# Attention stacks: constant rows from the input on GpSimd's queue, heads' outputs loaded further apart, projections moved, stores told later

## The chip, the core and the metric

The kernel runs on one core of a Trainium2 chip. A core has five engines that run side by side and meet only at semaphores: TensorE (PE in the profile; PEld is its loading of weights), VectorE (DVE), ScalarE (ACT), GpSimd (POOL) and SyncE (SP), which here only issues DMAs. Each engine takes its instructions in order, so an instruction that waits holds everything behind it on its engine. DMAs issued by SP and by GpSimd are carried out by 16 DMA engines, which all queues share. TensorE writes its results to PSUM, eight banks of 128 x 512 values; the other engines bring them to SBUF.

The metric is the device time of one execution in microseconds (us). The kernel before takes 858.89 us, the median of three runs (857.42 to 860.17).

## What is computed

One transformer block in float32, for 4 batches of 512 rows of 512 values: layer norm, attention with 32 heads of 16 values, causal, with a linear position bias for each head (ALiBi), projection and residual; then layer norm, a gated FFN with 1376 inner values, and residual.

```python
def attn(x):                                  # x: (4, 512, 512), already normed
    qkv = x @ w_attn + b_attn
    q, k, v = jnp.split(qkv, 3, axis=-1)      # each reshaped to (B, S, 32, 16)
    scores = jnp.einsum('bqhd,bkhd->bhqk', q, k) / 16
    bias = slopes[:, None, None] * rel[None, :, :]      # rel = key position - query position
    scores = jnp.where(causal, scores + bias, -inf)
    out = jnp.einsum('bhqk,bkhd->bqhd', softmax(scores), v).reshape(B, S, 512)
    return out @ w_proj + b_proj

def ffn(x):
    return (silu(x @ w_gate.T) * (x @ w_up.T)) @ w_down.T

x = x + attn(layernorm(x))
x = x + ffn(layernorm(x))
```

## The kernel before

**The order of the work is written out by hand.** Every step is put into a heap with a time (`at`, `spread`, `later`), and at the end the steps are taken out in order of that time and emitted. The unit is a slot: ten slots are one pass over one stack. All matmuls keep this order on TensorE, all DMAs keep it on SP, and instructions wrapped in `pin` keep it among themselves on their engine; other instructions of ScalarE, VectorE and GpSimd may be moved by the scheduler. `later(dt, send)` puts a store dt slots behind the step that made its data, so that SP reaches the store when the data is about ready and doesn't stand waiting.

**Stacks.** The attention goes over 32 stacks `su` = 0..31; unit `u = su // 2` is a quarter of a batch's heads (8 heads), and a stack holds 4 of them. A stack is an SBUF tile of 128 x 3 x 1024 values, four of them (`ST`) used in turn. Its planes hold q and k in pieces (rows 0 to 47 of each half of 64), the head's own slope and position rows (48 to 51), constant rows for the causal mask (52 to 63), and row `KM` = 59, into which the negated row maxima of the scores are written. So one matmul gives scores with bias, mask and maximum already in it. `load_stack` (L494) brings the q and k pieces, six DMAs of 128 KB from a DRAM tensor `qd`; `own_rows` (L479) brings the constant rows. Stacks 0 to 3 get these straight from the input `cst` on GpSimd's queue. For later stacks they come by SP, three DMAs each, from a DRAM tensor `cd`, which `load_cd` (L464) fills from `cst` with two DMAs on GpSimd's queue; the second of them is held by a small store of `c` (`gate`) so that it runs at a set point.

**One pass.** `pass_a` (L541) makes scores of a stack about two passes ahead and VectorE takes their row maxima (L557). `to_row` (L582) turns the maxima on TensorE and a DMA of GpSimd (L588) puts them into row `KM`. `pass_b` (L590) starts at slot `10 * su`: 11 fills (scores matmul, exp on ScalarE, L609, and the causal select of the diagonal block on GpSimd, L611), then values times weights in two parts (`av`, at 8.6 and 10.6 slots), and ScalarE's copy `ue` of the result (L631), which is stored to a DRAM tensor `ud`.

**GEMMs beside the passes.** The q and k projections of the next batch (`qk_steps`), its values (`v_steps`) and the output projection of an earlier batch (`proj_steps`) are spread between the matmuls of the passes, so that TensorE has work while VectorE and ScalarE work on scores. Each is 12 matmuls a tile (three products of high and low parts over four blocks of 128).

**Heads' outputs.** For a unit, `head_sums` loads the sums of the weights, `inverses` takes reciprocals and stores them (`rd`), `attn_heads` (L664) loads the unit's result `uc` and the reciprocals, broadcast, `rb`; `scaled_heads` (L674) multiplies them on GpSimd (L677) and splits the product on ScalarE (L680) and VectorE (L681) into `aT`. Four units make a batch, and then come `proj_steps`, four tiles a batch: `xr` is loaded from x, GpSimd adds the bias (L438), VectorE adds the product (L442), and the sum is stored to `x1d`, from which the FFN reads.

**Buffers.** `xt` (rows for a norm), `raw` (weights before their split), `ue`, `uc`, `rb`, `xr` and FFN's `sg` all share one tag, `x`, of nine buffers of 128 x 512 values. `xnT`, `c`, `aT` and `hl` share the tag `t4` of ten buffers. A buffer is free when the last reader of the tile before is done; for a stored tile that is when the store has landed. The Python line of an SP instruction or of a pinned one is often L77, that of the wrapper; the tile's name tells them apart.

The FFN goes over 4 batches and 11 blocks of the inner size, in slots 312 on; TensorE is its only limit.

Of the kernel before, what the change touches and what calls it, by code (L numbers as in the profile page):

```python
# [26 lines left out]
KM = 59  # L27
# [17 lines left out]
    'wp': 158.0,  # L45
# [20 lines left out]
def block_kernel(ctx, tc, x, wqk, wv, bqk, bv, wp, bp, wgu, wgul, wd, cst, out):  # L66
# [240 lines left out]

    cd = dr.tile([76, 4 * S], FR, name="cd")
# [53 lines left out]
    def qk_steps(u, qk):  # L362
# [13 lines left out]
        def done(p):  # L376
# [11 lines left out]
            def send():  # L388
                made.add(("qd", u, qk))
                sp.dma_start(qds[u][2 * qk : 2 * qk + 2].rearrange("n p c -> p n c"), f(c))  # L390
                if u == 3 and qk == 1:
                    load_cd(f(c)[0:1, 0, 0:1])

            later(1.0 if u < 4 else 3.0, send)
# [25 lines left out]
    def proj_steps(b, t):  # L420
# [19 lines left out]
        def done(p):  # L440
            xr = box["xr"]
            dve.tensor_tensor(xr, p, xr, ALU.add)  # L442

            def send():
                sp.dma_start(x1d[r0 : r0 + 128, :], xr)
                made.add(("x1", b, t))

            later(2.5, send)
# [15 lines left out]
    def load_cd(gate):  # L464

        sp.dma_start(f(cd[72:73, 0:1]), gate)
        pool.dma_start(cd[72:76], cst[72:76])
        pool.dma_start(cd[0:64], cst[0:64])

# [9 lines left out]
    def own_rows(su):  # L479
# [3 lines left out]
        for a in range(2):  # L483
            to = planes(st, a)
            if su < 4:
                to = st[64 * a : 64 * a + 64, 0 : 2 + a : 1 + a]
                pin(pool.dma_start(to[48:52], cst[r0 + 4 * a : r0 + 4 * a + 4].rearrange("r (n c) -> r n c", n=2)))
                pin(pool.dma_start(to[52:64], cst[64:76].rearrange("r (n c) -> r n c", n=2)))
            else:
                sp.dma_start(to[48:52], f(cd[r0 + 4 * a : r0 + 4 * a + 4]).rearrange("r (n c) -> r n c", n=2))  # L490
        if su >= 4:
            sp.dma_start(f(st)[KM : KM + 65 : 64, 0], f(cd[72:74, 0 : 2 * S]))

    def load_stack(su):  # L494
# [6 lines left out]
        if su >= 4:  # L501
            own_rows(su)
# [87 lines left out]
    def pass_b(su, t0):  # L590
# [26 lines left out]
        def av(*js):  # L617
# [11 lines left out]
            if js[-1] == NT - 1:  # L629
# [9 lines left out]
                later(3.0, send)  # L639
# [14 lines left out]
    def inverses(u):  # L654
# [7 lines left out]
        later(2.5, send)  # L662
# [34 lines left out]
    def xT_next(b, t0):  # L697
# [6 lines left out]
        else:  # L704
            spread(t0 - 36.0, t0 - 28.0, loads)
            spread(t0 - 22.0, t0 - 4.0, rest)
# [33 lines left out]
    for su in range(NS):  # L740
# [6 lines left out]
        if su + 4 < NS:  # L747
            at(t0 + 9.7, load_stack, su + 4)
    for b in range(B):
# [4 lines left out]
        if b + 1 < B:  # L754
            xT_next(b + 1, 10.0 * (t + PRM["xt"]) if b else 7.6)
            u = 4 * b + 4
            if b < 2:
# [13 lines left out]
    for b, first, gap, p0, p1_ in ((0, 175.5, 2.2, 192.0, 228.0), (1, 248.0, 2.3, 265.0, 290.0), (2, 273.0, 2.5, 291.0, 316.0)):  # L771
        for k in range(4):
            at(first + gap * k, attn_heads, 4 * b + k)
            at(first + 7.5 + gap * k, scaled_heads, 4 * b + k)
# [76 lines left out]
    def ffn(b, times):  # L851
# [5 lines left out]
        spread(t0 - (23.0 if b else 21.0), t0 - 18.0, loads)  # L857
        spread(t0 - 15.5, t0 - 8.0, rest)
# [130 lines left out]
```

## Time and profile before

| | |
|---|---|
| median of three runs | 858.89 us (857.42 to 860.17) |
| the profiled execution | 856.17 us; its span, first to last instruction, 854.4 us |
| PE busy | 822.4 us, so idle 32.0 us |
| of it idle in 0 to 20 us / 60 to 80 / 280 to 300 | 8.0 / 2.3 / 1.8 |
| idle in 380 to 400 / 400 to 420 / 420 to 440 / 440 to 460 | 1.9 / 7.5 / 3.6 / 2.4 |
| mean granted clock of TensorE in these four | 0.83 / 0.87 / 0.79 / 0.91 |
| VectorE, ScalarE, GpSimd busy | 474.8 / 358.7 / 228.5 us |
| VectorE's row maxima, L557: 512 reductions and 512 reads | 245.9 + 72.5 us |
| ScalarE's exp, L609 | 352, 191.7 us |
| DMA | 99.54 MB, 116 GB/s over the span |
| st<-cd on SP | 84 issues; 56 of 32 KB and 28 of 8 KB |
| st<-mt on GpSimd | 32 issues of 8 KB, 5.5 us to landing |

How to read it: times in the trace count from the first instruction. A stack's maxima row (st<-mt) marks the passes: 69.35, 80.30, 91.43 us and so on stand at slots 10.6, 20.6, 30.6; slot 100.6 is at 176.3 us, 200.6 at 298.7, 250.6 at 368.0 and 300.6 at 446.5. A pass takes 11 us where the GEMMs beside it are thin and 13 to 15 where they are dense. In a list of waits the columns are the engine and line that waited, what it waited for, the sum, the count and the longest, all in us. In an order of time they are start, duration, engine, line, operation and, in brackets, the idle time before it and what ended it. The granted clock is that of TensorE as a share of its full speed.

### The profile page before, as it was taken

The numbers are of one execution on the slowest core, as the hardware profiler recorded it, in microseconds if no ns is written. First come the engines' busy times: TensorE is split into PE (matmuls) and PEld (weight loads), VectorE is DVE, ScalarE is ACT, GpSimd is POOL, SyncE is SP. The second block draws the span as 40 slices with busy tenths as digits, with TensorE's granted clock in tenths as the row PEclk, the third lists the DMA queues.
The fourth block names the chain that finished last, engine by engine and source line by source line (L and its number), as shares of the span: only waits on it lengthen the run. The fifth ranks groups of instructions, "written<-read, shape, count | busy, mean of one in ns | idle before, by whom it ended". The sixth has DMA issues, their size and how long they took to land.

```text
span 854.4 us, 13257 instructions
## 1 busy us (share of the span) xinstructions
PE 822.4 (96%) x4448; PEld 630.6 (74%) x4448; DVE 474.8 (56%) x1438; ACT 358.7 (42%) x678; POOL 228.5 (27%) x519
## 2 busy tenths in 40 slices
PE   6999999999999999999499999999999999999998
PEld 4876777777777577757366788878887888878886
DVE  6798897778877776667384554443114311431112
ACT  4646666566667555555266632221112111121111
POOL 5824443333445443344463211000000000000000
PEclk9999999999999999998799999999999999999999
DMA  6586886578867776668654543312000210110101
GB/s 234 126 184 122 180 183 125 102 153 190 182 141 176 191 171 153 161 153 180 189 164 137 191 122 124 139 37 84 16 25 25 74 25 12 25 63 13 37 1 50
DMA packets 53990, 99.54 MB, mean 116 GB/s; under 512 B 12954, under 2 KB 13210, under 8 KB 53730
## 3 DMA queue, kind: packets, MB, share of 16 engines
q1 hardware_dynamic: 52194, 96.80, 45.6%
q0 software_dynamic: 1728, 1.89, 1.1%
q8 instruction: 36, 0.59, 0.3%
q14 instruction: 32, 0.26, 0.1%
HBM read 65.61 MB, written 33.33 MB: 116 GB/s over the span
## 4 chain that ended last, share of the span: by engine, by line
PE 89%; DMA 3%; ACT 2%; issue 2%; DVE 1%; POOL 1%; SPq 0%; ACTq 0%; POOLq 0%; DVEq 0%
PE bank L85 87%; PE bank L88 2%; DMA ud<-ue 1%; ACT P L609 1%; DMA rb<-rd 1%; DMA xt<-in_x 1%; DMA st<-mt 1%; POOL P L611 0%; POOL uc L677 0%; DVE r L139 0%; ACT c L379 0%; DVE r L77 0%; DVE xt L144 0%; SPq L77 0%; ACT L879 0%
## 5 line engine op out<-in xcount | busy, mean ns | idle before, releaser
L557 DVE CUSTOM_DVE_ANT_0 bank<-bank,mask_t 128x128 f32<-128x128 f32 (+3 forms) x512 | 245.9, 507 | 81.3 <-PE bank L85 75.3
L85 PE MATMUL bank<-xnT,wf 128*128 128x512 f32 (+1 forms) x1056 | 258.5, 393 | 0.0
L85 PE MATMUL bank<-st 128*128 128x512 f32 (+3 forms) x896 | 240.6, 343 | 13.9 <-ACT ue L631 12.6
L609 ACT ACTIVATE P<-bank 128x512 f32<-128x512 f32 (+1 forms) x352 | 191.7, 560 | 115.3 <-PE bank L85 109.0
L85 PEld LDWEIGHTS bank<-xnT,wf 128*128 128x128 f32 (+1 forms) x1056 | 195.5, 186 | 45.3 <-issue 0.2
L85 PEld LDWEIGHTS bank<-st 128*128 128x128 f32 x896 | 159.8, 192 | 43.2 <-ACT ue L631 13.5
L611 POOL TENSOR_SCALAR_AFFINE_SELECT P<-P 128x128 f32<-128x128 f32 (+2 forms) x352 | 123.2, 353 | 186.6 <-ACT P L609 180.2
L883 DVE TENSOR_TENSOR sg<-sg,bank 128x512 f32<-128x512 f32 (+1 forms) x44 | 30.3, 688 | 196.4 <-PE bank L85 195.3
L85 PE MATMUL bank<-xnT,wqk_t 128*128 128x512 f32 x384 | 139.4, 402 | 0.0
L85 PE MATMUL bank<-wf,hl 128*128 128x512 f32 (+1 forms) x528 | 131.4, 393 | 0.0
L85 PEld LDWEIGHTS bank<-wf,hl 128*128 128x128 f32 (+1 forms) x528 | 98.8, 188 | 22.0
L879 ACT ACTIVATE sg<-bank 128x512 f32<-128x512 f32 (+1 forms) x44 | 26.4, 599 | 156.7 <-PE bank L85 156.3
L85 PEld LDWEIGHTS bank<-xnT,wqk_t 128*128 128x128 f32 x384 | 71.3, 188 | 22.5 <-issue 11.9
L85 PE MATMUL bank<-P,v 128*32 128x512 f32 (+3 forms) x1024 | 83.8, 439 | 2.3 <-POOL P L611 2.2
L85 PE MATMUL bank<-wrow_t,aT 128*128 128x512 f32 x192 | 76.2, 419 | 0.4 <-ACT P L609 0.4
L885 ACT CAST hl<-sg 128x512 fp32r<-128x512 f32 (+1 forms) x44 | 27.4, 622 | 115.8 <-DVE sg L883 115.8
L557 DVE DVE_READ_ACCUMULATOR2_ANT M<- 128x1 f32 x512 | 72.5, 142 | 0.0
L85 PE MATMUL bank<-wrow_t,xnT 128*128 128x512 f32 x192 | 67.5, 417 | 0.3 <-DVE xnT L77 0.2
L85 PEld LDWEIGHTS bank<-P,v 128*32 128x32 f32 x1024 | 26.8, 109 | 43.3 <-issue 21.8
L132 POOL TENSOR_SCALAR ve<-mv 128x4 f32<-128x4 f32 x7 | 1.6, 230 | 211.5 <-DVE mv L128 211.5
L85 PEld LDWEIGHTS bank<-wrow_t,aT 128*128 128x128 f32 x192 | 37.6, 200 | 9.3 <-issue 3.1
L886 DVE TENSOR_TENSOR hl<-sg,hl 128x512 fp32r<-128x512 f32 (+1 forms) x44 | 30.6, 697 | 24.3 <-ACT hl L885 24.1
(79 smaller groups left out, 508.7 us busy)
## 6 DMA issues: line engine op xcount, KB each, us to landing
st<-qd SPq DMA_DIRECT2D x180, 128.0 KB
qd<-c SPq DMA_DIRECT2D x30, 512.0 KB
ud<-ue SPq DMA_DIRECT2D x32, 256.0 KB
raw<-in_wgu SPq DMA_DIRECT2D x20, 256.0 KB
xt<-in_x SPq DMA_DIRECT2D x16, 256.0 KB
uc<-ud SPq DMA_DIRECT2D x16, 256.0 KB
rb<-rd SPq DMA_DIRECT2D x16, 256.0 KB
xr<-in_x SPq DMA_DIRECT2D x16, 256.0 KB
```

Of the source, the lines that this page charges most:

```text
L85: tc.keep_in_program_order(nc.tensor.matmul(*args, **kw))
L88: tc.keep_in_program_order(nc.tensor.transpose(*args))
L132: pin(pool.tensor_scalar(ve, box["mv"][:, :, 1], EPS, None, ALU.add))
L557: dve.tensor_tensor_reduce(s, s, mask_t[:, S - w : S], -1.0, 3.0e38, ALU.add, ALU.min, m[:, n : n + 1])
L609: act.activation(pt, p[:, :w], AF.Exp)
L611: pool.affine_select(d, d, pattern=[[0, len(heads)], [1, 128]], compare_op=ALU.is_ge, fill=0.0, base=0, channel_multiplier=-1)
L879: act.activation(sg[:m], p, AF.Silu)
L883: dve.tensor_tensor(sg[:m], sg[:m], p, ALU.mult)
L885: act.copy(hl[:m, 0, :], sg[:m])
L886: dve.tensor_tensor(hl[:m, 1, :], sg[:m], f(hl[:m, 0, :]), ALU.subtract)
```

## The change

1. `cd` and `load_cd` go. `own_rows` takes the rows of every stack from `cst` on GpSimd's queue: three DMAs a stack for stacks 4 to 31, pinned, in place of SP's three. It is a step of its own at slot `t0 + 8.55`, behind the last fill (8.5) of the pass that used the stack's tile; `load_stack` moves from `t0 + 9.7` to `t0 + 10.3`.
2. Heads' loads of batches 0, 1, 2 begin at slots 102, 182, 246 (175.5, 248, 273 before), 5, 5 and 6 slots apart (2.2, 2.3, 2.5), each scaled 8.0 slots after its load (7.5). Their projections go to slots 127 to 148, 207 to 228 and 274 to 298 (192 to 228, 265 to 290, 291 to 316). The projection's weights are loaded from slot 84 (158).
3. The q and k projections of batch 2 are dealt out in three stretches, as those of batch 3 were, from slot 102 on instead of 94.5.
4. Loads of rows for the norms of batches 2 and 3 come 26 to 20 slots ahead of their turns (36 to 28), the norm 17 to 4 ahead (22 to 4). FFN batch 0's loads come 24 to 20 ahead (21 to 18), its norm 18 to 10 (15.5 to 8).
5. Stores are told later: `qd` 4.5 slots after its data (3.0; batch 0 as before 1.0), `x1d` 4.5 (2.5), `ud` 4.0 (3.0; the last as before), `rd` 4.5 (2.5; the last as before).

```diff
-    'wp': 158.0,
+    'wp': 84.0,
-    cd = dr.tile([76, 4 * S], FR, name="cd")
...
                 sp.dma_start(qds[u][2 * qk : 2 * qk + 2].rearrange("n p c -> p n c"), f(c))
-                if u == 3 and qk == 1:
-                    load_cd(f(c)[0:1, 0, 0:1])
-            later(1.0 if u < 4 else 3.0, send)
+            later(1.0 if u < 4 else 4.5, send)
...
                 made.add(("x1", b, t))
-            later(2.5, send)
+            later(4.5, send)
...
-    def load_cd(gate):
-        sp.dma_start(f(cd[72:73, 0:1]), gate)
-        pool.dma_start(cd[72:76], cst[72:76])
-        pool.dma_start(cd[0:64], cst[0:64])
...
         for a in range(2):
-            to = planes(st, a)
+            to = st[64 * a : 64 * a + 64, 0 : 2 + a : 1 + a]
+            pin(pool.dma_start(to[48:52], cst[r0 + 4 * a : r0 + 4 * a + 4].rearrange("r (n c) -> r n c", n=2)))
             if su < 4:
-                to = st[64 * a : 64 * a + 64, 0 : 2 + a : 1 + a]
-                pin(pool.dma_start(to[48:52], cst[r0 + 4 * a : r0 + 4 * a + 4].rearrange("r (n c) -> r n c", n=2)))
                 pin(pool.dma_start(to[52:64], cst[64:76].rearrange("r (n c) -> r n c", n=2)))
-            else:
-                sp.dma_start(to[48:52], f(cd[r0 + 4 * a : r0 + 4 * a + 4]).rearrange("r (n c) -> r n c", n=2))
         if su >= 4:
-            sp.dma_start(f(st)[KM : KM + 65 : 64, 0], f(cd[72:74, 0 : 2 * S]))
+            pin(pool.dma_start(st[KM : KM + 65 : 64, 0], cst[72:74, 0 : 2 * S]))
...
-        if su >= 4:
-            own_rows(su)
...
                     sp.dma_start(uds[u][128 * s : 128 * s + 128, :], ue)
-                later(3.0, send)
+                later(4.0 if su < 31 else 3.0, send)
...
-        later(2.5, send)
+        later(4.5 if u < 15 else 2.5, send)
...
-            spread(t0 - 36.0, t0 - 28.0, loads)
-            spread(t0 - 22.0, t0 - 4.0, rest)
+            spread(t0 - 26.0, t0 - 20.0, loads)
+            spread(t0 - 17.0, t0 - 4.0, rest)
...
-            at(t0 + 9.7, load_stack, su + 4)
+            at(t0 + 8.55, own_rows, su + 4)
+            at(t0 + 10.3, load_stack, su + 4)
...
-            if b < 2:
+            if b < 1:
...
-    for b, first, gap, p0, p1_ in ((0, 175.5, 2.2, 192.0, 228.0), (1, 248.0, 2.3, 265.0, 290.0), (2, 273.0, 2.5, 291.0, 316.0)):
+    for b, first, gap, p0, p1_ in ((0, 102.0, 5.0, 127.0, 148.0), (1, 182.0, 5.0, 207.0, 228.0), (2, 246.0, 6.0, 274.0, 298.0)):
         for k in range(4):
             at(first + gap * k, attn_heads, 4 * b + k)
-            at(first + 7.5 + gap * k, scaled_heads, 4 * b + k)
+            at(first + 8.0 + gap * k, scaled_heads, 4 * b + k)
...
-        spread(t0 - (23.0 if b else 21.0), t0 - 18.0, loads)
-        spread(t0 - 15.5, t0 - 8.0, rest)
+        spread(t0 - (23.0 if b else 24.0), t0 - (18.0 if b else 20.0), loads)
+        spread(t0 - (15.5 if b else 18.0), t0 - (8.0 if b else 10.0), rest)
```

## The prediction

> **What bounds the kernel now.** I read the page first (busy time, slices), then PE's waits, then 2 us windows around the bad slices, then SP and ACT there.
>
> ```profile
> PE 822.4 (96%) x4448; PEld 630.6 (74%) x4448; DVE 474.8 (56%) x1438; ACT 358.7 (42%) x678; POOL 228.5 (27%) x519
> PE   6999999999999999999499999999999999999998
> PEclk9999999999999999998799999999999999999999
> ```
>
> PE is the bound: 96% busy, and the sum of its work is the same after the change. Only its idle 32.0 us and slow-clock stretches can be won. Slice 20 (406 to 427 us) is the one hole inside the run.
>
> ```profile
> PE bank L85 <- ACT ue L631: 12.6, 2, 11.1
> PE bank L88 <- DVE xt L77: 7.7, 2, 6.8
> PE bank L85 <- POOL P L611: 2.2, 2, 1.7
> PE bank L88 <- DVE xt L144: 2.1, 1, 2.1
> ```
>
> PE's own waits: the largest is for the copy of a stack's heads out of PSUM (ue). The order of time shows what held that copy:
>
> ```profile
> 411.81 7.49 SPq L77 DMA_DIRECT2D st<-qd  x6
> 419.42 0.35 SPq L77 DMA_DIRECT2D x1d<-xr  x1
> 422.94 0.59 ACT L631 COPY ue<-bank 128x512 f32<-128x512 f32 x1 [11.89 <-issue]
> ```
>
> ACT waits for a buffer. Buffers of tag x (nine) serve ue, xr, uc, rb, xt and raw. One is freed by a store of xr, which SP issues at 419.42, after six stack loads that took it 7.49 us; 3.5 us later, the time such a store needs to land, ue runs. SP's waits there are for heads' loads (rb<-rd, uc<-ud). Batch 1's four heads' loads, 2.3 slots apart, hold eight of the nine buffers, and batch 2's follow 18 slots later.
>
> ```profile
> 384.00:386.00 2.00, 1.64 (x5) 0.52 0.64 172
> 386.00:388.00 2.00, 2.00 (x6) 0.50 0.36 68
> 424.00:426.00 2.00, 2.00 (x7) 0.50 0.74 271
> 426.00:428.00 2.00, 2.00 (x7) 0.50 0.65 250
> 448.00:450.00 2.00, 0.00 (x0) 1.00 0.57 199
> 452.00:454.00 2.00, 2.00 (x8) 0.58 0.42 130
> ```
>
> Columns: window, its length, PE busy (count), granted clock, DMA share, GB/s. After each hole PE runs at half clock for 4 to 8 us.
>
> **The change, against the profiled execution's 856.2 us** (span 854.4 and 1.8 around it; 2.7 under the median of 858.9).
>
> Removed losses:
> 1. *Heads' loads spread, batches 1 and 2.* Between 380 and 392 us PE is idle 1.9 and loses 3.3 to the clock (5.6 busy at 0.5 is 2.8 lost, 2.0 at 0.78 is 0.4). From 412 to 430: idle 11.1, and 2.4 to the clock. Both waits are for ue's buffer. With gaps of 5 to 6 slots and scaling 8 slots after the load, two pairs are alive: four or five buffers. All 18.7 go; ends 10 and 18.7.
> 2. *FFN's first norm.* PE idles 2.4 at 448 (xt L144), then 4.0 us at about 0.57, 1.7 lost. Its x1d loads were issued at 428 and 435, behind the congestion. I take 3 of 4.1 (0 to 4.1).
> 3. *Heads of batch 0.* GpSimd waits 2.61 for rb at 281 and PE 1.69 for its selects: 1.7 back (0 to 1.8).
> 4. *No cd.* GpSimd's queue stands 2.38 us for the gate:
>
> ```profile
> 64.65 0.55 POOL L467 DMA_DIRECT2D cd<-in_cst  x1 [2.38 <-DMA cd<-c]
> 65.19 0.65 POOL L611 TENSOR_SCALAR_AFFINE_SELECT P<-P 128x512 f32<-128x512 f32 x1
> ```
>
> The select behind it is held 1 to 2 us; PE idles 2.3 between 60 and 80. I take 1.5 (0 to 2.3). The other cd copy, 512 KB at 2.46 us, competes with the first loads (DMA at 423 GB/s from 4 to 6 us), where the chain waits 5.92 us for xt; 0.5 MB at that rate is 1.2: take 1 (0 to 1.5).
> 5. SP issues 84 fewer (st<-cd, median 0.512, 43 us over the run, 1.5 a stack). SP ran ahead of PE outside the holes: 0.
>
> Sum removed: 25.9.
>
> Added:
> 6. *Three DMAs a stack on GpSimd, 28 stacks.* The st<-mt issue there costs 0.575 (longest 0.794): 1.7 us a stack, 49 in all. GpSimd is 27% busy, but is a queue; the order matters. In the stack near 110 us:
>
> ```profile
> 109.36 0.60 ACT L609 ACTIVATE P<-bank 128x512 f32<-128x512 f32 x1 [1.12 <-PE bank L85]
> 110.03 0.64 POOL L611 TENSOR_SCALAR_AFFINE_SELECT P<-P 128x512 f32<-128x512 f32 x1 [1.31 <-ACT P L609]
> 111.50 0.42 PE L85 MATMUL bank<-P,v 128*32 128x256 f32 x4
> ```
>
> The rows wait for the last fill's matmul (done at 109.36). Issued then, they end at 111.1, the select at 111.7, against the matmul at 111.50: 0.2 to 0.3 late. Issued behind the select, they end at 112.4 and delay the next stack's first select 0.5, which nobody needs for 8 us. So 0 to 8 in all; I take 3, as the rows come later in the program than that select. Next in the queue is st<-mt (lands in 5.5, needed 9.4 slots later): 0. The stack loads, now told at 10.3 slots instead of 9.7 plus 1.5 of row issues, start no later: 0.
>
> The DMA page of the Trainium skill (DMA: Bandwidth & Descriptors, "SWDGE vs HWDGE vs iDMA") says that GpSimd writes its descriptors to SBUF, which VectorE in its two-port modes locks it out of. By that the issues could be longer beside a busy VectorE; the 32 st<-mt issues, beside a VectorE 80 to 90% busy, show 0.575 to 0.794, so the trace bears out no more than 0.2.
>
> 7. *Work moved forward leaves less beside the late stacks.* A stack pass without GEMM: its scores and fills are 20 matmuls' worth of 512 columns, at 20.00/88 = 0.227 (FFN windows) 4.5; values 1.7 and 0.9; turn 0.3: 7.4 on PE. DVE needs (245.9+72.5)/32 = 9.95. So 2.6 idle per uncovered ten slots. Until now projections of two batches (12 matmuls a tile, 10.9 a batch) lay between slots 265 and 316; now one, 274 to 298. Slots 262 to 274 hold no GEMM: 1.2 x 2.6 = 3.1. From 298 to 312 only fills and values remain: PE 4.9 a pass, ACT 191.7/32 + 0.8 = 6.8: 1.4 x 1.9 = 2.7. Slots 120 to 127 and 200 to 207 have one qk at 2.4 a pass: about 1. Sum 6.8 (2 to 12; below if FFN's transposes cover the end).
> 8. *Heads at new places.* Twelve products of uc and rb on GpSimd; if rb is late, selects stand behind. Four cost 1.8 before in a burst; spread out, 2 for all (0 to 5.4).
> 9. *Later stores.* ue's buffer is held one slot longer, xr's two, qd's c 1.5: hidden as long as the ring has room. I count at most eight of nine near slot 140 (four xt, three xr, one ue): 0, up to one hole as in 1. Weights' loads at 84 instead of 158: four buffers for 7 slots, no other burst there: 0.
> 10. *xt loads of batches 2 and 3 ten slots later, their norm five later, batch 2's qk in three stretches.* No instruction is added. The last load is told 3 slots (3.3 us) before the first statistics, but those take the first tile, 8 slots old; cover is VectorE's scores, and where a tile lands late (5.92 us at the start, the longest xt row), its statistics, pinned on VectorE, hold the reductions behind them: 0, at most 2 a batch. FFN batch 0's loads told 3 slots earlier: counted in 2.
>
> Added: 11.8. Net 14.1: 856.2 becomes 842.1. Against the median (plus 2.7) it is 844.8; I say **844**.
>
> **Rivals.**
> - *The hole moves* (0.20). Slots 102 to 160 now carry heads, projection and batch 3's xt loads; at 180 to 240 us the DMA share already is 0.81 to 0.83, more than the 0.73 where ue stalled. Against it: 145 to 208 GB/s there, while windows of 380 to 420 occur. One hole like 412 to 430 costs 13.5: 857; two, slower.
> - *Slower: GpSimd's queue* (0.15). If the three issues go ahead of the last select and of a late rb product, the values' matmul waits up to 0.9 a stack (1.7 less 0.8 of slack): 28 x 0.9 = 25, 22 more than taken: 866. It turns slower above 17/28 = 0.6 a stack. For it: PE's weight loads already wait for selects 36 times, 13.9 us. Against: the program's order.
> - *Late stacks starve PE to half clock* (0.10). A gap of 1.55 us in a stretch 61% busy (380 to 384) was enough; here 74% busy for 12 slots. Two episodes of 2.4 to 3.3: 850. The Trainium skill (TensorE: Matmul & The Clock Gate, "Part 1: The HAM clock gate") states an idle window of about 3.4 us before the clock halves; by that none of these small gaps would count and this rival falls. The trace disagrees as far as gaps go: 1.55 and 2.4 us were followed by half clock.
>
> **How the numbers follow.** Forecast 0.55 (own range 836 to 851, from the ends of 1, 6 and 7 not all at once), all faster. Half clock 0.10, faster. Hole moved 0.20: faster 0.05, within 0.3% 0.04, slower 0.11. GpSimd 0.15, slower. A difference under 0.3% (2.6 us) can't be told from none, as runs of one kernel spread that much. Faster 0.70, same 0.04, slower 0.26. The range 832 to 864 leaves 0.05 under it (losses all gone, late stacks covered) and 0.13 over it.
>
> **What would show it.** Right: no PE wait for ue above 1 us, clock 1.0 between 370 and 450; POOL near 277 us; no cd; PE's 40 slices full but for small losses where slots 262 to 274 lie (near 370 to 390 us). Wrong: PE waiting for POOL P in nearly every stack (step 6); ACT's ue, or POOL's xr or uc, waiting for DMA at 180 to 250 us (step 9, ring); late slices under 8 (step 7).

## The result, and the profile after

The changed kernel takes 855.82 us (median of 20 runs, 853.96 to 858.70) against 859.82 us for the kernel before in the same comparison (20 runs, 856.28 to 861.63). The ratio is 0.9963, with a 95% interval from 0.9950 to 0.9975: faster by 0.37%, where the prediction said 1.7% (844 of 858.9). The profiled execution has a span of 854.3 us, against 854.4 before; that both spans are about equal although the medians differ by 4.0 us shows how far single executions scatter, so gains below are read from the ratios, and causes from the places in the trace.

The page of the changed kernel, busy time and slices:

```profile
PE 819.6 (96%) x4448; PEld 629.5 (74%) x4448; DVE 472.0 (55%) x1438; ACT 358.1 (42%) x678; POOL 274.4 (32%) x601
PE   6999999989999988999798999999999999999998
PEclk9999999999999989999999999999999999999999
```

The one deep hole of before (slice 20, a 4) is gone. In its place stand a 7 near 406 to 427 us and several 8s. GpSimd has 45.9 us more work (228.5 to 274.4), as step 6 counted (49). PE is idle 34.7 us, no less than before (32.0), only elsewhere: 4.6 us between 180 and 200, 5.7 between 300 and 340, and 9.2 between 400 and 480, besides the 8.0 at the start.

PE's own waits in the changed kernel (us in total, times, longest):

```profile
PE bank L85 <- DVE M L542: 9.6, 4, 4.6
PE bank L88 <- DVE xt L77: 7.9, 1, 7.9
PE bank L85 <- DMA st<-qd: 6.2, 4, 2.4
PE bank L88 <- DVE M L542: 4.2, 4, 1.5
PE bank L88 <- DVE xt L144: 1.3, 1, 1.3
PE bank L85 <- POOL P L596: 1.3, 2, 0.7
```

There is no wait for `ue` any more (12.6 us before) and hardly one for the selects (1.3 after 2.2). New are waits for the row maxima `M` and for the loads of the stacks. The maxima are made by VectorE, and the order of time shows why VectorE was late:

```profile
192.10 0.35 DVE L641 RECIPROCAL rc<-lc 128x32 f32<-128x32 f32 x1 [5.37 <-DMA st<-qd]
193.16 1.44 PE L85 MATMUL bank<-st 128*128 128x256 f32 x3 [4.58 <-DVE M L542]
```

A reciprocal of the sums, pinned in VectorE's order, stood 5.37 us, and the maxima behind it kept PE idle 4.58 us. The chain of waits, over the same stretch, names the load (start, us, what):

```profile
173.00 9.27 DMA ud<-ue
182.34 9.68 DMA lc<-ud
...
196.54 6.08 DMA uc<-ud
202.63 8.06 DMA st<-qd
```

A store of 256 KB took 9.27 us to land, then a load of 16 KB (`lc`) 9.68 us. (The bracket of the reciprocal above names a stack load; the chain names `lc`, whose sums the reciprocal reads.) These are transfers that drag. The same chain shows a second effect: in its last two lines a stack load starts when a `uc` has landed, and that load is the eighth DMA that SP issues after the `uc`. Near 310 us the same happens with a `uc` of 9.37 us, and SP's six stack loads there took 7.84 us to issue, as the 7.49 us of the kernel before. So a slow transfer also stops SP itself.

What the DMA engines did meanwhile, in windows of 2 us (window, length, PE busy and count, granted clock, DMA share, GB/s), changed kernel:

```profile
178.00:180.00 2.00, 2.00 (x19) 1.00 0.67 182
180.00:182.00 2.00, 2.00 (x19) 1.00 0.52 169
182.00:184.00 2.00, 2.00 (x22) 1.00 0.54 196
...
186.00:188.00 2.00, 2.00 (x11) 1.00 1.08 118
188.00:190.00 2.00, 0.58 (x3) 1.00 1.04 140
190.00:192.00 2.00, 0.00 (x0) 1.00 0.51 92
192.00:194.00 2.00, 0.84 (x3) 0.77 0.45 102
194.00:196.00 2.00, 2.00 (x7) 0.50 0.66 228
```

Two things can be read here. Ahead of the hole the share is 0.52 to 0.54, about half of the 16 engines; the last loads that SP had issued were two pairs of `uc` and `rb`, at 170.75 to 176.99 us, with one store of `ue` and one of `qd` between them, and it issued nothing from then to 182.34. And in the hole the share is 0.45 to 0.51 again, while PE waits for a transfer. The last group of experiments takes this up.

### The profile page after: what moved, and what is told of

It reads as the page before. It is cut to its first block, busy times and chain, and to the rows that moved or that the text cites. A ratio compares the mean times of both kernels' runs of the same rounds, so it can differ in the third digit from the quotient of the medians.

```text
span 854.3 us, 13248 instructions
## 1 busy us (share of the span) xinstructions
PE 819.6 (96%) x4448; PEld 629.5 (74%) x4448; DVE 472.0 (55%) x1438; ACT 358.1 (42%) x678; POOL 274.4 (32%) x601
## 4 chain that ended last, share of the span: by engine, by line
PE 81%; DMA 10%; DVE 5%; issue 1%; ACT 1%; SPq 1%; POOL 0%; POOLq 0%; DVEq 0%; ACTq 0%
PE bank L85 79%; DMA st<-qd 4%; PE bank L88 2%; DMA lc<-ud 2%; DMA ud<-ue 2%; DVE bank L542 2%; DMA uc<-ud 2%; SPq L77 1%; ACT P L594 0%; DVE M L542 0%; DVE r L77 0%; DMA raw<-in_wv 0%; DVE st L127 0%; ACT wf L241 0%; DVE aT L666 0%
## 5 line engine op out<-in xcount | busy, mean ns | idle before, releaser
L542 DVE CUSTOM_DVE_ANT_0 bank<-bank,mask_t 128x512 f32<-128x512 f32 (+3 forms) x512 | 245.0, 507 | 88.0 <-PE bank L85 81.9
L85 PE MATMUL bank<-xnT,wqk_t 128*128 128x512 f32 x384 | 142.9, 406 | 0.0
L85 PE MATMUL bank<-wrow_t,aT 128*128 128x512 f32 x192 | 71.9, 397 | 0.0
L85 PE MATMUL bank<-wrow_t,xnT 128*128 128x512 f32 x192 | 65.0, 409 | 0.0
L85 PEld LDWEIGHTS bank<-wrow_t,xnT 128*128 128x128 f32 x192 | 36.0, 192 | 8.6 <-issue 2.5
```

The costliest lines, as they stand in the source:

```text
L85: tc.keep_in_program_order(nc.tensor.matmul(*args, **kw))
L542: dve.tensor_tensor_reduce(s, s, mask_t[:, S - w : S], -1.0, 3.0e38, ALU.add, ALU.min, m[:, n : n + 1])
```

## Experiments

All ratios are to the kernel before, measured in the same comparison. Line numbers are each kernel's own.

### The parts of the change, one at a time

**Spread alone.** The kernel before with the heads' loads 5 slots apart, close to their old places:

```diff
-((0, 175.5, 2.2, 192.0, 228.0), (1, 248.0, 2.3, 265.0, 290.0), (2, 273.0, 2.5, 291.0, 316.0))
+((0, 168.0, 5.0, 192.0, 228.0), (1, 241.0, 5.0, 265.0, 290.0), (2, 267.0, 5.0, 291.0, 316.0))
-            at(first + 7.5 + gap * k, scaled_heads, 4 * b + k)
+            at(first + 8.0 + gap * k, scaled_heads, 4 * b + k)
```

> The kernel before, with the heads' loads of batches 0 to 2 five slots apart (from slots 168, 241, 267) and scaled 8 slots after, everything else as before, projections too. If the burst alone made the hole (step 1 of the prediction): 845 to 850, with no wait for ue over 1 us. If the late stretch is too full whatever the spacing, because loads for projections, heads and the FFN meet there: 854 to 862, with holes elsewhere between 380 and 460 us.

Measured: 850.37 us, 0.9929 [0.9908, 0.9949]. Two lines of the diff give twice the gain of the whole change. The three largest of its PE waits, beside the start's:

```profile
PE bank L88 <- DVE xt L144: 4.9, 1, 4.9
PE bank L85 <- DVE xr L442: 4.6, 2, 3.0
PE bank L85 <- DMA uc<-ud: 2.1, 1, 2.1
```

There is no wait for `ue`, as step 1 said. (That the burst alone makes this wait is not shown: it falls to 1.0 us as well in a run below that keeps the burst and takes the rows over GpSimd's queue.) But 18.7 us of loss gone should have given more than 7.2 us of time. PE is still idle 11.7 us between 380 and 460 us, after 15.4 in the kernel before, and 9.5 of that are the waits for `xt` and `xr`. The wait for a heads' load (`uc`) lies near 280 us, where the kernel before was idle 1.8.

**Spread and moved.** In addition the new places of heads, projections and their weights, and batch 2's q and k projections in three stretches:

```diff
-((0, 168.0, 5.0, 192.0, 228.0), (1, 241.0, 5.0, 265.0, 290.0), (2, 267.0, 5.0, 291.0, 316.0))
+((0, 102.0, 5.0, 127.0, 148.0), (1, 182.0, 5.0, 207.0, 228.0), (2, 246.0, 6.0, 274.0, 298.0))
-    'wp': 158.0,
+    'wp': 84.0,
-            if b < 2:
+            if b < 1:
```

> The kernel before with heads and projections at the places of the kernel after (gaps, scaling, projection weights from slot 84, batch 2's q and k in three stretches), without its rows, stores and norm times. The spread alone gave 0.9929. Theory: the move costs what the spread won, since early passes take 11 us and leave the DMA engines no room: 854 to 860, with holes between 170 and 220 and 290 and 340 us. If the move is not to blame but the rows or the later stores are: 846 to 851.

Measured: 861.32 us, 1.0042 [1.0018, 1.0066]. The move costs 1.1% and turns the gain into a loss. PE waits in it 3.9 us for `ud`, 3.8 for selects, 3.4 for `qd`, 3.0 for the maxima and 2.7 for `uc`: nothing single, all of it transfers or what stands behind them. Where it loses can be told, by windows of 20 us:

```profile
180.00:200.00 20.00, 17.73 (x113) 0.94 0.79 185
200.00:220.00 20.00, 14.15 (x80) 0.93 0.71 181
...
300.00:320.00 20.00, 16.90 (x114) 1.00 0.78 174
```

PE is idle 8.3 us between 180 and 240 us and 4.4 between 300 and 340, where the run with spread alone has no idle time at all. Between 380 and 460 us it is idle 4.8 us, less than the 11.7 of spread alone.

**Half of the move.** Batch 0's heads from 168, batch 1's from 212, batch 2's from 250:

```diff
-((0, 168.0, 5.0, 192.0, 228.0), (1, 241.0, 5.0, 265.0, 290.0), (2, 267.0, 5.0, 291.0, 316.0))
+((0, 168.0, 5.0, 192.0, 222.0), (1, 212.0, 5.0, 238.0, 262.0), (2, 250.0, 6.0, 278.0, 302.0))
```

> The kernel before, with the heads' loads spread (5, 5 and 6 slots apart) at places between its own and the change's: from slot 168 (batch 0), 212 and 250, where the run that only spreads has 168, 241, 267 (0.9929) and the run that spreads and moves has 102, 182, 246 (1.0042). Theory A, the cost of moving is paid wherever a pair of head loads meets a stack's loads without other work for TensorE near by, so it falls about in proportion to the distance moved: half of the 11 us, 0.997 to 1.000 of the kernel before. Theory B, the cost belongs to a few places alone (the fifth unit's heads at 182 to 197 and the loads around slot 100 to 120): batch 1 and 2 lie past the first of them and batch 0 is unmoved, so it is 0.992 to 0.994, as spread alone.

Measured: 853.05 us, 0.9948 [0.9927, 0.9969], between the two theories and nearer to spread alone. Distance by itself doesn't set the price.

**Later stores.** Spread alone, with the stores told later as in the change (`qd` and `x1d` at 4.5, `ue` at 4.0, `rd` at 4.5 slots):

```diff
-            later(1.0 if u < 4 else 3.0, send)
+            later(1.0 if u < 4 else 4.5, send)
...
-            later(2.5, send)
+            later(4.5, send)
...
-                later(3.0, send)
+                later(4.0 if su < 31 else 3.0, send)
...
-        later(2.5, send)
+        later(4.5 if u < 15 else 2.5, send)
```

> The kernel before with heads' loads spread (as in the run of the spread alone, 850.4) and with the later stores of the kernel after. If later stores are free: 848 to 853. If they cost, because a sum's load waits for a store told a slot later and holds buffers longer: 855 or more, with waits for reciprocals or for ue.

Measured: 852.25 us, 0.9936 [0.9914, 0.9959], against 0.9929 without. Later stores cost nothing that can be told.

**Rows on GpSimd's queue**, in three schedules. First alone, in the kernel before (`cd` and `load_cd` go, `own_rows` as in the change, stack loads at 10.3 slots):

```diff
-                sp.dma_start(to[48:52], f(cd[r0 + 4 * a : r0 + 4 * a + 4]).rearrange("r (n c) -> r n c", n=2))
+            pin(pool.dma_start(to[48:52], cst[r0 + 4 * a : r0 + 4 * a + 4].rearrange("r (n c) -> r n c", n=2)))
...
-            sp.dma_start(f(st)[KM : KM + 65 : 64, 0], f(cd[72:74, 0 : 2 * S]))
+            pin(pool.dma_start(st[KM : KM + 65 : 64, 0], cst[72:74, 0 : 2 * S]))
...
-            at(t0 + 9.7, load_stack, su + 4)
+            at(t0 + 8.55, own_rows, su + 4)
+            at(t0 + 10.3, load_stack, su + 4)
```

> The kernel before, with the constant rows alone taken over GpSimd's queue at slot 8.55 and the stack loads told at 10.3; heads, projections and stores as before. If the rows cost nothing, or give the cd gate's time back (1.5 us): 856 to 860, with the hole for ue near 412 us still there. If three more issues a stack hold the selects (rival GpSimd's queue): 863 or more, with PE waiting for POOL P in most stacks. The start: idle in 0 to 20 us stays 8.0 if the cd copy was not what held the first loads.

Measured: 858.72 us, 1.0006 [0.9975, 1.0036]. PE's waits of this kernel:

```profile
PE bank L85 <- POOL P L597: 7.6, 6, 3.2
PE bank L85 <- DMA st<-qd: 4.6, 1, 4.6
```

Against what I had expected, the wait for `ue` fell from 12.6 to 1.0 us, yet selects (GpSimd behind a late `rb`, for which it waits 30.1 us here) and a stack load took the place. Then the other way, the changed kernel with its rows back on SP, through `cd`:

```diff
-            at(t0 + 8.55, own_rows, su + 4)
-            at(t0 + 10.3, load_stack, su + 4)
+            at(t0 + 9.7, load_stack, su + 4)
```

> The kernel after with the constant rows back on SP from cd and stack loads at 9.7, all else as after. If the rows on GpSimd are free (as in the kernel before, where they alone gave 1.0006): 853 to 858. If they cost something where the heads come early: 846 to 851, and PE's waits for the selects, for st<-qd or for the reciprocals are smaller.

Measured: 859.40 us, 1.0025 [1.0004, 1.0046], against 0.9963 with the rows on GpSimd. And spread alone together with the rows on GpSimd, nothing moved (to the kernel before, the diff of the rows above and this):

```diff
-((0, 175.5, 2.2, 192.0, 228.0), (1, 248.0, 2.3, 265.0, 290.0), (2, 273.0, 2.5, 291.0, 316.0))
+((0, 168.0, 5.0, 192.0, 228.0), (1, 241.0, 5.0, 265.0, 290.0), (2, 267.0, 5.0, 291.0, 316.0))
```

> Spread alone (0.9929) and the constant rows on GpSimd's queue, nothing else of the change. Theory A, the rows' gain of 0.6% (moved schedule with rows on GpSimd 0.9963, with rows on SP 1.0025) is there only because the moved heads crowd SP's queue: 0.992 to 0.994 here, as the rows alone did nothing (1.0006). Theory B, three DMAs a stack fewer on SP are worth their 0.6% in any schedule whose ue hole is gone: 0.986 to 0.988, near 846 us.

Measured: 850.49 us, 0.9899 [0.9878, 0.9921], against 0.9929 for spread alone; the intervals overlap, so this lies between the two theories. The rows on GpSimd, with the later place of the stack loads that belongs to them, are a gain of 0.6% in the moved schedule, and of 0.3%, if any, in the unmoved one.

### Wrong turns: the order of waiting

**Reciprocals later.** Since the hole at 188 us stands behind a reciprocal, the changed kernel with the first three batches' reciprocals told 5 slots later:

```diff
-        at(20.0 * u + 33.0, inverses, u)
+        at(20.0 * u + (38.0 if u < 12 else 33.0), inverses, u)
```

> The kernel after, with the reciprocals of units 0 to 11 told 5 slots later (slot 20u+38 instead of 20u+33). Theory A: the two largest new holes (4.6 us at 189, 3.3 us at 304, each followed by half clock) are VectorE standing in order at a reciprocal whose sums (lc) have not landed, because the heads' loads now lie between; told later, VectorE no longer stands: 7.9 us of idle and about 4 of clock back, 844 to 849. Theory B: the DMA engines are simply too full there, and PE will wait for the stack loads instead: 853 to 858, with PE's waits for st<-qd grown by what the waits for DVE lost.

Measured: 860.42 us, 1.0050 [1.0024, 1.0075]: worse than the changed kernel. The waits only moved. Its PE waits for stack loads and selects, 6.2 and 1.3 us in the changed kernel:

```profile
PE bank L85 <- DMA st<-qd: 8.5, 4, 3.1
PE bank L85 <- POOL P L596: 7.0, 5, 2.8
```

**Heads right behind the stack loads.** Two units' loads, 0.2 slots apart, directly after a stack's loads, so that they wouldn't stand ahead of any:

```diff
-            at(first + gap * k, attn_heads, 4 * b + k)
-            at(first + 8.0 + gap * k, scaled_heads, 4 * b + k)
+            t = (100.4, 180.4, 250.4)[b] + 10.0 * (k // 2) + 0.2 * (k % 2)
+            at(t, attn_heads, 4 * b + k)
+            at(t + 8.0 + 0.8 * (k % 2), scaled_heads, 4 * b + k)
```

> The kernel after, with each batch's heads' loads told directly behind a stack's loads (two units at slots 100.4 and 110.4, 180.4 and 190.4, 250.4 and 260.4), scaled 8 and 8.8 slots later, projections where the kernel after has them. Theory A (what hurts is where in a pass a head's load stands, because SP's stack loads wait until the eighth DMA before them has landed, and a head's uc takes 9 us): PE's waits for st<-qd (6.2 us in all) go, since a full pass lies between; the waits for the reciprocal can stay: 848 to 853. Theory B (bytes and descriptors in that stretch): bursts of two units make it no better, 855 to 862.

Measured: 865.91 us, 1.0123 [1.0078, 1.0167]. Stack loads are waited for less (2.4 us for 6.2), as meant, but selects more:

```profile
PE bank L85 <- POOL P L596: 13.2, 7, 5.2
```

GpSimd waited 42.4 us for `rb` in this kernel. Whoever is put behind waits: it is not the order that is wrong, some transfer is too slow.

### Which transfer, and why

**No `rb`.** The changed kernel without that load; the result is multiplied by itself, so the division by the sums is left out:

```diff
-        rb = com.tile([128, S], F32, tag="x", bufs=PRM["xb"], name="rb")
-        sp.dma_start(rb, rd.rearrange("h (o q) -> h o q", o=1).broadcast_to((8, 16, S)))
-        heads[u] = uc, rb
+        heads[u] = uc, uc
```

> The kernel after without the loads of rb: the heads' outputs are multiplied by themselves instead of by the reciprocals, so the division by the sums is left out; 16 loads of 256 KB fewer, all instructions of the other engines kept. Theory A (the DMA engines are full: a stack's six loads alone keep them at a share of 1.0 for 6.5 of 11 us, and the heads' loads come on top): the waits for the reciprocal and for st<-qd shrink to a half or less, 845 to 850. Theory B (the order on SP and the place of the GEMMs make the holes, not the load on the DMA engines): 852 to 857.

Measured: 839.74 us, 0.9783 [0.9751, 0.9816]: 1.8% under the changed kernel for sixteen loads. PE's waits for stack loads fall to this (6.2 in the changed kernel):

```profile
PE bank L85 <- DMA st<-qd: 0.8, 1, 0.8
```

But this run takes away bytes, a place on SP, a buffer and a wait at once. The next ones tell those apart. `rb` reads 8 rows, each 16 times, and `uc` reads 8 runs of 16 rows, so the outermost count of both accesses is 8. The Trainium skill (DMA: Bandwidth & Descriptors, "Why a DMA increments its semaphore by 16 and not by 1") says that a DMA runs on as many engines as the largest number up to 16 that divides the outermost counts of both sides, on SP's queue the lowest-numbered ones. By that `uc` and `rb` would run on the same 8 engines, and the share of 0.52 to 0.54 above would be those 8.

**`rb` from sixteen rows.** The changed kernel, the reciprocals stored twice, the bytes into `rb` the same:

```diff
-            rds[u] = dr.tile([8, S], F32, tag="rd", bufs=16, name="rd")
-            sp.dma_start(rds[u].rearrange("h (a q) -> (h a) q", a=16), rc)
+            rds[u] = dr.tile([16, S], F32, tag="rd", bufs=16, name="rd")
+            for k in range(2):
+                to = rds[u].rearrange("(h k) (a q) -> h k a q", k=2, a=16)[:, k]
+                sp.dma_start(to, rc)
...
-        sp.dma_start(rb, rd.rearrange("h (o q) -> h o q", o=1).broadcast_to((8, 16, S)))
+        sp.dma_start(rb, rd.rearrange("h (o q) -> h o q", o=1).broadcast_to((16, 8, S)))
```

> The changed kernel with the reciprocals stored twice, as 16 rows, and rb read from the 16 rows, each repeated 8 times, where it was read from 8 rows, each repeated 16 times: one more DMA of 16 KB a unit on SP, the same bytes into rb. The run without rb was 16 us faster than the changed kernel (839.7). Theory A, an access whose outermost step counts 8 runs on 8 of the 16 DMA engines, and it is this crowding that makes rb dear (by the Trainium skill, DMA: Bandwidth & Descriptors, the number of engines is the largest up to 16 that divides the outermost counts; no run here has shown it): GpSimd's wait for rb falls from 20.1 us to under 10, and the time to 0.982 to 0.991. Theory B, what is dear is rb's place in SP's order or its wait for the reciprocals: no change, 0.995 to 1.000, the additional store costing up to 2 us.

Measured: 849.95 us, 0.9901 [0.9884, 0.9918]. The time is as theory A had it, but GpSimd's wait for `rb` did not fall (21.3 us, after 20.1): what gains are the transfers beside and behind it.

**Stored twice, read as before.** The control for the additional store:

```diff
+            kept.append(dr.tile([8, S], F32, tag="rd2", bufs=16, name="rd2"))
+            sp.dma_start(kept[-1].rearrange("h (a q) -> (h a) q", a=16), rc)
```

> The changed kernel with the reciprocals stored twice, into two tensors of 8 rows, of which only the first is read: the additional store of the run with sixteen rows, without its other reading. SP's DMAs then come round to each other in the same order as in that run. Theory A, the reading made the gain: 0.996 to 0.999, the store costing 0 to 2 us. Theory B, the additional DMA shifted which DMA waits for which: 0.989 to 0.992, as the run with sixteen rows.

Measured: 856.57 us, 0.9990 [0.9967, 1.0013]. The store alone gives nothing, so the reading does.

**`rb` from 128 rows of x.** The division by the sums is left out:

```diff
+        sp.dma_start(rb, x[128 * u : 128 * u + 128, :])
```

> The changed kernel with rb loaded from 128 rows of the input x in place of the reciprocals, so that the division by the sums is left out: as many bytes into the same buffer at the same place in SP's order, but with no reciprocal to wait for, no row read twice, and an outermost count of 128. If rb's bytes and its place on SP are what costs (theory B), the time is 0.994 to 0.998, as the changed kernel. If the reading of few rows or the wait for the reciprocals is (theories A and C), 0.979 to 0.986, near the run without rb; of these two, the run with sixteen rows gains along with this one only by A.

Measured: 849.63 us, 0.9903 [0.9886, 0.9920], the same as with sixteen rows. So neither the wait for the reciprocals nor the repeated reading of a row costs anything that can be told beyond the form of the access.

**`uc` from x as well.** The attention's outputs are left out altogether:

```diff
+        sp.dma_start(uc, x[128 * ((u + 1) % 16) : 128 * ((u + 1) % 16) + 128, :])
```

> The run with rb from the input (0.9903), and the other load of a heads' pair, uc, also from 128 rows of the input x in place of the 8 runs of 16 rows in ud; scaling and projection then work on the input's rows, the attention's outputs being left out. Same bytes, same places on SP, but no wait for the stored outputs and an outermost count of 128 where ud's reading has 8. Theory A, what makes the heads' pairs dear is that both readings have an outermost count of 8: uc brings as much again as rb, 0.982 to 0.986. Theory B, bytes and places on SP: 0.989 to 0.992, unchanged.

Measured: 838.81 us, 0.9781 [0.9759, 0.9803]. All bytes and all places on SP are kept, and the time is that of the run without `rb`. What remained open was `uc`'s wait for the attention's outputs, which this run dropped too.

**Rows outermost.** The whole computation, with the partitions' order turned from (head, row) to (row, head). Both loads then have an outermost count of 16, from the same tensors, and no DMA is added or moved; the projection's weights and the values' bias are loaded in the same order:

```diff
-        sp.dma_start(uc, u3[:, 0:16, :])
+        sp.dma_start(uc, u3[:, 0:16, :].rearrange("h r q -> r h q"))
...
-        sp.dma_start(rb, rd.rearrange("h (o q) -> h o q", o=1).broadcast_to((8, 16, S)))
+        sp.dma_start(rb, rd.rearrange("(o h) q -> o h q", o=1).broadcast_to((16, 8, S)))
...
+                sp.dma_start(box[n], wp[r0 : r0 + 128, :].rearrange("(h r) c -> r h c", r=16))
...
-        pin(sp.dma_start(bv_t, bv))
+        pin(sp.dma_start(bv_t, bv.rearrange("(h r) u -> r h u", r=16)))
```

> The changed kernel with the order of the partitions turned: the row of a head is the outer count (16) and the head the inner (8), in uc, rb, the projection's weights and the values' bias, so that uc and rb are read from the same tensors with an outermost count of 16; no DMA more, none moved, all of it computed. Theory A, the outermost count of 8 is what makes both readings dear: rb gave 0.6% and uc from the input a further 1.2%, so 0.977 to 0.983. Theory B, uc's gain in that run came from no longer waiting for the attention's outputs, and only rb's reading counts here: 0.988 to 0.992.

Measured: 838.88 us, 0.9775 [0.9748, 0.9802], 1.9% under the changed kernel (0.9775 / 0.9963 = 0.981). The form of the two readings was the cause. The page of this kernel:

```profile
PE 816.4 (97%) x4448; PEld 628.2 (75%) x4448; DVE 472.0 (56%) x1438; ACT 358.3 (43%) x678; POOL 276.0 (33%) x601
PE   6998999999999999999989999999999999999998
PEclk9999999999999999999999999999999999999999
```

Its PE waits, of those shown above for the changed kernel:

```profile
PE bank L88 <- DVE xt L77: 8.3, 1, 8.3
PE bank L88 <- DVE M L546: 3.0, 4, 1.2
PE bank L85 <- DVE M L546: 1.7, 2, 1.3
...
PE bank L85 <- DMA st<-qd: 0.2, 1, 0.2
```

And its windows at the place of the hole:

```profile
178.00:180.00 2.00, 2.00 (x15) 1.00 1.05 195
180.00:182.00 2.00, 2.00 (x18) 1.00 1.07 406
...
188.00:190.00 2.00, 2.00 (x14) 1.00 1.08 142
190.00:192.00 2.00, 2.00 (x22) 1.00 1.00 218
192.00:194.00 2.00, 2.00 (x14) 1.00 1.05 387
194.00:196.00 2.00, 2.00 (x24) 1.00 1.15 318
```

Here the share is 1.0 or more (0.83 in the one window from 182), and PE is busy all the time. The changed kernel had 0.80 on average from 170 to 200 us at 164 GB/s; this one has 1.05 at 209. The trace also has every packet that the DMA engines moved, and the pieces of `uc` and `rb` are packets of 2 KB. Counting all packets of 1 KB and more, mostly 8 or 9 are on their way at the same time between 180 and 184 us in the changed kernel, and mostly 16 or 17 between 180 and 182.5 us in this one; a packet of 2 KB takes 84 ns (median) in both. So each packet went as fast there as here, but only half as many went side by side. This agrees with the rule of the Trainium skill above; which of the 16 engines they were, the trace doesn't show.

**Turned, and nothing moved.** The same four edits in the run that has spread and rows on GpSimd but the old places; to the changed kernel with rows outermost, its heads differ by this:

```diff
-((0, 102.0, 5.0, 127.0, 148.0), (1, 182.0, 5.0, 207.0, 228.0), (2, 246.0, 6.0, 274.0, 298.0))
+((0, 168.0, 5.0, 192.0, 228.0), (1, 241.0, 5.0, 265.0, 290.0), (2, 267.0, 5.0, 291.0, 316.0))
```

> The same turned order where the heads stay at the old places: spread from 168, 241 and 267, constant rows on GpSimd's queue (0.9899 without the turn, 0.9863 with rb alone read from 16 rows). Theory A: below 0.9863, at 0.977 to 0.983, and then moving the heads costs nothing once they are read so. Theory B: 0.984 to 0.989.

Measured: 839.45 us, 0.9783 [0.9757, 0.9808]. The largest of its PE waits beside the start's:

```profile
PE bank L88 <- DVE xt L144: 4.9, 1, 4.9
PE bank L85 <- DVE xr L443: 1.0, 1, 1.0
```

Once the loads are wide, the moved schedule takes no more time than the unmoved one (0.9775 and 0.9783), where the same step without the turn cost 0.6% (0.9899 to 0.9963). The two also differ by the later stores and norms: the wait for `xt L144` is 4.9 us here and 1.3 in the moved one, so some 3 us of a price of moving may be hidden behind that. With only `rb` read from sixteen rows in this schedule, the reciprocals stored twice as above:

```diff
+        sp.dma_start(rb, rd.rearrange("h (o q) -> h o q", o=1).broadcast_to((16, 8, S)))
```

> The kernel before with the heads' loads spread (from 168, 241, 267), the constant rows on GpSimd's queue, and rb read from reciprocals stored twice as 16 rows; nothing moved. Spread and rows alone gave 0.9899, the sixteen rows took 0.62% off the changed kernel (0.9963 to 0.9901). Theory A, the eight-row reading costs wherever heads' loads lie among stack loads: 0.982 to 0.986, near 844 us. Theory B, it costs only where the heads' loads have been moved into batches 0 to 2's stack loads at the wrong places: 0.988 to 0.991, the same as without.

Measured: 846.18 us, 0.9863 [0.9837, 0.9888], 0.4% from `rb` (the intervals with and without it overlap) and then 0.8% from `uc`.

**Sums and reciprocals turned too.** The 16 KB loads `lc` and stores `rd` with an outermost count of 16:

```diff
-        sp.dma_start(lcs[u], uds[u].rearrange("(h r) q -> h r q", r=32)[:, 16, :].rearrange("h (a q) -> h a q", a=16))
+        sp.dma_start(lcs[u], uds[u].rearrange("(h r) q -> h r q", r=32)[:, 16, :].rearrange("h (a q) -> a h q", a=16))
...
-            sp.dma_start(rds[u].rearrange("h (a q) -> (h a) q", a=16), rc)
+            sp.dma_start(rds[u].rearrange("h (a q) -> a h q", a=16), rc)
```

> The run before it with the 16 KB loads of the sums and stores of the reciprocals turned in the same way (outermost count 16 in place of 8). Theory A: these are 128 pieces of 128 bytes each, small beside the 256 KB of uc and rb, but the sums' load took 9 to 10 us on the chain of waits: 0 to 3 us faster than the run before it. Theory B: their time is the wait behind other loads: within 0.2% of it.

Measured: 840.18 us, 0.9796 [0.9764, 0.9828], no difference. `lc` took 9.68 us because of what was ahead of it, not by its own form: with `uc` and `rb` turned and `lc` as it was, no reciprocal of the moved kernel waits as much as 0.2 us for its sums, where two stood 5.37 and 4.09 us.

The two kernels with rows outermost, moved and unmoved, beat both the kernel before and the changed one. What was not run is the kernel before with rows outermost and nothing else, so how much of its own hole at 412 us came from the same cause stays open.

## Why the prediction was right and wrong

The sign was right, and the time lies in the range. The size was off: a gain of 3 to 4 us where 14.9 were forecast. Two steps failed, step 1 by its size and step 8 by its price, and behind both, as far as the runs tell, stands the same omission: a pair of heads' loads was counted as buffers held and as a wait of GpSimd, and the time for which it keeps the DMA engines was put at nothing. Along the runs, spread alone gave 7.2 us (steps 1 and 3: 20.4), the move cost some 9.7 (steps 7 and 8: 8.8), later stores and norms gave some 1.5, within scatter (steps 2 and 9: 3), and the rows on GpSimd gave some 5.3 (steps 4 to 6: a loss of 0.5). That the whole is a gain at all is luck: the rows brought some 6 us more than their steps had. By its own steps:

- **Step 1 (spread) failed by its size.** What it wanted gone is gone: PE no longer waits for `ue`, the clock is 1.00 from 380 to 440 us. But "all 18.7 go", with 10 as the lower end, came to 7.2; 11.6 us of waits on `xt`, `xr` and `uc` stand in that run's list, of which only the 2.1 for `xt` were there before. With both loads turned and nothing moved, the wait for `uc` is gone and that for `xr` 1.0, and the turn is worth 1.2% there (0.9899 to 0.9783), some 10 us. That this is what step 1 lacked fits in size, and is not shown for each us; the 4.9 for `xt` stay.
- **Step 2 (the FFN's norm)** was of the right kind: the wait for `xt L144` is 4.9 us where only spread was done, 1.3 in the changed kernel.
- **Step 3** holds: no idle time between 280 and 300 us.
- **Step 4 (no `cd`) gave nothing** where 2.5 were taken. PE is idle 8.0 us in the first 20, as before, and 2.85 between 60 and 80 instead of 2.3: with the gate gone it waits for the maxima there. The rows-only run, at 1.0006 [0.9975, 1.0036], can't tell 2.5 us of gain from none.
- **Step 5 (84 issues fewer on SP, 0)** was too low for the moved schedule: the rows' way is worth 0.6% there. Whether by the issues, or because those loads read 4 rows or fewer each and so may also have run on few engines, was not tried.
- **Step 6 (GpSimd's queue, +3)** is inside its ends, at its lower one: PE's waits for selects fell to 1.3 us in the changed kernel; the 7.6 of the rows-only run are six waits, with GpSimd behind a late `rb`, and not one in nearly every stack. The rival of GpSimd's queue falls with it.
- **Step 7 (late stacks, +6.8) is not seen.** Between 380 and 460 us the moved run has 4.8 us of idle time where spread alone has 11.7. With rows outermost the moved kernel has 6.2 there and the unmoved one 7.5; of the 6.2, PE waits 1.5 us for maxima, which is what the step described. In the changed kernel the idle time is 14.9 from 300 to 480, most of it gone with the loads turned.
- **Step 8 (heads at new places, +2, ends 0 to 5.4) failed by its price.** At the new places PE is idle 12.7 us in the moved run (180 to 240 and 300 to 340 us), where spread alone has none; in the changed kernel it is 10.6, and with both loads turned 0.4. The step was priced by GpSimd's wait for a late `rb`; the price was paid by everything else in flight: stores of `ue`, the sums' loads, stack loads.
- **Step 9 (later stores, 0)** was right where it was tried, in the unmoved schedule: 0.9936 against 0.9929.
- **Step 10** was not tried by itself; moved with and without the later stores and the later norms gave 1.0025 and 1.0042, which can't be told apart.

**The rival that came true was "the hole moves"**, at its place: the hole at 188 to 194 us lies near slot 113, and the rival had named slots 102 to 160. That its price came out too (857 for 855.8) is luck: that hole is 4.6 us of idle time and 1.4 lost to the clock, not 13.5, others stand at 300 to 340 us, and step 1 gave less than the rival took for it. The rival was held at 0.20 by this sentence: "145 to 208 GB/s there, while windows of 380 to 420 occur". That took the GB/s for the room that was left. The share said otherwise, and even 0.81 to 0.83 said it badly, for a mean over 16 engines can hide that one half is full and the other idle. The rival of half clock in the late stacks shows in small only: the clock is 0.91 between 440 and 460 us and 1.00 from 320 to 440.

A single pair of heads' loads can be seen by itself in the kernel before, at 354 us:

```profile
354.09 0.64 SPq L77 DMA_DIRECT2D uc<-ud  x1
354.77 0.60 SPq L77 DMA_DIRECT2D rb<-rd  x1
```

```profile
358.00:360.00 2.00, 2.00 (x11) 1.00 0.54 180
360.00:362.00 2.00, 2.00 (x13) 1.00 0.20 61
```

The first fence is SP's order of time, the second windows of 2 us. When the stack loads ahead are through, the pair runs at a share of 0.54, and is done about 6 us after its issue: so this could have been read before the result. With it, step 8 would have been: 12 pairs of 512 KB on half of the engines, each some 6 us in which whatever needs those engines is delayed, now among stack loads that fill all 16.

## What to carry to other kernels

- Read the DMA share before the GB/s, and look for a share that stands at a simple fraction while something waits: here about 0.5 with a transfer outstanding meant that the shape of the access, not the bytes, set its time. Turning the order of the partitions, so that the outermost count of both loads was 16 and not 8, gave 1.9% with no DMA moved.
- If every rearrangement of loads moves a wait to another place (reciprocals, stack loads, selects), stop rearranging and make the slow transfer faster. Leaving out one load showed its worth in one run, and reading the same bytes from elsewhere showed why.

## What the runs showed of the hardware that I had not expected

- **The outermost count of the two 256 KB loads set how many packets ran side by side.** Read as 8 runs, `uc` and `rb` went with 8 or 9 packets at a time, at a share of 0.52 to 0.54 and 169 to 196 GB/s; with 16, it was 16 or 17 packets, 1.0 and more, and up to 406 GB/s, in the same place. One packet of 2 KB took 84 ns in both.
- **A share of 1.0 can go with few GB/s.** While mainly a stack's six loads are on their way (186 to 190 us above), the engines are full at 118 to 140 GB/s. These write 16 partitions in pieces of 4 KB; why they are slow was not tried.
- **A small transfer can take as long as what is ahead of it**: 9.68 us for 16 KB. Widening its own access changed nothing (0.9796 after 0.9783); widening the loads ahead took the wait away.
- **In these kernels SP stops at the eighth DMA after one that has not landed**: 7.84 us for six issues that take 2.64 to 2.67 where nothing is late.
